# Attention and a top-2 mixture of experts on one core: a new order for the steps that find the row maxima

## The chip, the core and the metric

The kernel runs on one core of a Trainium2 chip. TensorE (PE) multiplies matrices, with weight loads shown apart as PEld; VectorE (DVE), ScalarE (ACT) and GpSimd (POOL) do elementwise work; SyncE (SP) issues DMAs. The metric is the device time of one execution in microseconds (us); lower is better.

## The reference

The input `x` has 8 batches of 1024 tokens of 256 numbers. All data are 32-bit floats.

```
x = x + layernorm(attention(layernorm(x)))      # 16 heads of 16, causal
x = x + layernorm(moe(layernorm(x)))            # 8 experts, top 2 per token

attention:  q, k, v = Wq x, Wk x, Wv x
            score = q k^T / 4, -inf above the diagonal
            out = Wo (softmax(score) v)
moe:        the 2 best experts of 8 by softmax(router)
            gate = min(gate, 7), up clipped to -7..7
            act = (up + 1) * gate * sigmoid(1.702 gate), then the down projection
            sum of the two, weighted by the router's scores
```

## The kernel before, in words

The program has two parts. The first, some 1400 us long, is the attention of all batches with the router; the second runs the experts over 142 tiles of 256 tokens. The change lies in the first part.

The attention is cut into 32 **units**: 8 batches times 4 groups of 4 heads (`u` counts units, `g = u % 4` is the group). A unit's 1024 x 1024 causal scores are computed twice. First, `maxima_tiles(u)` computes them with the queries in partitions (PSUM tile `sa`, line 689) and reduces them to a maximum for each row. Then the negated maxima go, transposed, into a spare row of the queries `qP`, so that when `values_tiles(u)` computes the scores again, with the keys in partitions (PSUM tile `sb`, line 784), the maximum is already subtracted and ScalarE has only to take the exponential (`pT`, line 792). The second pass of a unit runs one unit later than the first: in each iteration of the loop over `u`, the maxima of unit `u` and the exponentials of unit `u - 1` are worked at together.

**Steps and pairs.** Both passes go through 9 steps (`STEPS`, lines 631 to 643, `k` = 0 to 8), and each step handles two heads at a time (`pair` 0 and 1), the other pass taking the other two heads. A unit has so 18 pair-steps. In a pair-step TensorE makes 2 x 512 columns of scores for the maxima and 2 x 512 for the exponentials, in four different groups of 32 rows of the array; then half a step's products of `pT` with the values (`av`, line 821) for the step two before; then pieces of other work. A step is one of three kinds:

- EDGE: one query tile against the 512 keys at the diagonal. VectorE adds a mask and takes the maximum in one instruction per head (line 699).
- TWO: two query tiles whose causal widths add up to 512 (128 + 384, or 256 + 256). VectorE takes the maximum over the full blocks (line 714 or 720), and ScalarE copies the diagonal blocks out of PSUM into the tile `edge` (line 724). When both pairs are done, GpSimd masks `edge` (line 738) and VectorE reduces it (line 743).
- WHOLE: one query tile of the second 512 rows against all the first 512 keys; one reduction (line 705).

The kinds, in the order of `k`, are EDGE, TWO, TWO, EDGE, TWO, WHOLE, WHOLE, WHOLE, WHOLE. The TWO at `k` = 2, called "both" here, has one tile in each half (chunk `c`) of the rows. In the second pass every step but WHOLE has one or two diagonal blocks that GpSimd masks (line 801).

**The rows.** `rows(c)` sends the maxima of chunk `c` off when its last step has been counted: VectorE reduces and negates (`nm`, line 655), TensorE transposes (`nmps`, line 658), ScalarE copies (`nmT`, line 660), and four DMAs on SyncE's queue write the rows of `qP` (line 662). The chunk 0 rows can leave after "both"; the chunk 1 rows after the last WHOLE. The next unit's loop needs chunk 0 at step 0 and chunk 1 at step 2.

**The order of the work.** TensorE, VectorE, ScalarE and SyncE follow the order of the source. Pieces of other work (projections `pjq` and `pjk`, values `vps`, output projection `yps`, transposes `xps`, `aps`, `x2ps`, `avt`, the layer norms, the router) are placed by a small planner. Each pair-step earns credit for every engine (lines 1194 to 1200: 2.26 us less what the step itself takes), and a piece is placed when its turn has come and the engines that it needs have credit. Large pieces (1.75 us of TensorE) are placed ahead of a step's first `av` half (line 1206); when one is, and the step of `av` has one chunk only, both halves move to the second pair (`whole`). In pump, called at the end of each pair-step, small ones follow. `rows`, the mask jobs and `normalize` are "urgent" and come first.

**Buffers.** `sa` has two buffers of two PSUM banks. The pool `ps_b` has three of one bank: a pair-step's two `sb` tiles take two, and each piece of other work takes one.

**SyncE's queue.** `spread(u + 1)` (line 612) copies the next unit's queries and keys into `qP` and `kP`: two DMAs of zeros (line 617) and eight of data (line 620). It is called at the start of a unit, or at step 7 for the last group of a batch (line 1170). The queue holds also the `rows` DMAs, the loads of `x` (at step 5 of a batch's first unit) and the stores `x1d` (line 903).

Of the kernel before, what the change touches and what calls it, by code (L numbers as in the profile page):

```python
# [24 lines left out]
def piece(pe=0.0, dve=0.0, act=0.0, pool=0.0, after=0):  # L25


    return (pe, dve, act, pool), after
# [30 lines left out]
def attn_moe_kernel(  # L59
# [159 lines left out]
    def in_order(put, scatter=False):  # L219

        if free[0]:
            return
        for before_it in fixed if scatter else fixed + loose:
            tc.add_manual_dep(
                put.ins, before_it,
                mybir.DependencyInfo(mybir.DependencyClass.NoSync, mybir.DependencyReason.DATA),
                reason="order of the source",
            )
        if scatter:
            loose.append(put.ins.name)  # L230
        else:
            fixed[:], loose[:] = [put.ins.name], []
# [175 lines left out]
    with ExitStack() as attn:  # L408
# [219 lines left out]
        n = QC // P  # L628
        assert n == 4 and NC == 2
        WHOLE, EDGE, TWO = range(3)  # L630
        STEPS = []
# [10 lines left out]
        STEPS += [(WHOLE, [(n + i, 0, QC)], [(1, i, 0)]) for i in range(n)]  # L642
        K = len(STEPS)

        def maxima_tiles(u):

            b, g = divmod(u, NG)
            qP, kP = qPs[u % NU], kPs[u % NU]
            mx = mxs[u % 2]
            edges = {}  # L650

            def rows(c):
                yield piece(dve=0.2)
                nm = ap2.tile([P, HG, n], F32, tag="nm", name=f"nm_{u}_{c}")
                nc.vector.tensor_reduce(nm, mx[:, :, ts(c, n), :], AX.X, ALU.max, negate=True)
                yield piece(pe=0.15, act=0.3, after=1)
                ps = ps_b.tile([HG * n, P], F32, tag="b", name=f"nmps_{u}_{c}")
                nc.tensor.transpose(ps, nm.rearrange("p h i -> p (h i)"), ident)
                nmT = ap2.tile([HG * n, P], F32, tag="nmT", name=f"nmT_{u}_{c}")
                nc.scalar.copy(nmT, ps)  # L660
                for hh in range(HG):
                    nc.sync.dma_start(
                        out=qP[hh * HS + DH : hh * HS + DH + 1, ts(c, QC)].rearrange(
                            "o (i q) -> o i q", q=P
                        ),
                        in_=nmT[ts(hh, n), :],
                    )

            left = [
                sum(c in {i // n for i, _, _ in tiles} for _, tiles, _ in STEPS)  # L670
                for c in range(NC)
            ]

            def of_two(k):

                (i, _, w), (i2, _, _) = STEPS[k][1]
                return slice(i, i2 + 1, i2 - i), w == P

            def pair_of_heads(k, pair):
                kind, tiles, _ = STEPS[k]  # L680
                ps = ps_a.tile([P, 2, QC], F32, tag="a", name=f"sa_{u}_{k}_{pair}")

                def scores(hh, part):
                    if part == len(tiles):
                        return
                    i, c, w = tiles[part]
                    at = sum(t[2] for t in tiles[:part])
                    r = ds((2 * pair + hh) * HS, HS)
                    nc.tensor.matmul(  # L689
                        ps[:, hh, ds(at, w)], lhsT=qP[r, ts(i, P)], rhs=kP[r, ds(c * QC, w)],  # L690
                        start=True, stop=True,
                    )

                def reduce():
                    heads = ts(pair, 2)
                    i, c, w = tiles[0]
                    if kind == EDGE:
                        for hh in range(2):
                            nc.vector.tensor_tensor_reduce(  # L699
                                out=ps[:, hh, :], in0=ps[:, hh, :], in1=cmask,  # L700
                                scale=1.0, scalar=NEG, op0=ALU.add, op1=ALU.max,
                                accum_out=mx[:, 2 * pair + hh, i, 0:1],
                            )
                    elif kind == WHOLE:
                        nc.vector.tensor_reduce(mx[:, heads, i, 2:3], ps, AX.X, ALU.max)  # L705
                    else:
                        both, short = of_two(k)
                        if k not in edges:
                            edges[k] = ap2.tile(
                                [P, HG, 2, P], F32, tag="edge", name=f"edge_{u}_{k}"  # L710
                            )
                        blocks = ps.rearrange("p h (b k) -> p h b k", k=P)
                        if short:
                            nc.vector.tensor_reduce(  # L714
                                mx[:, heads, tiles[1][0], 0:1], ps[:, :, P : 3 * P],
                                AX.X, ALU.max,
                            )
                            at = blocks[:, :, 0:4:3, :]
                        else:
                            nc.vector.tensor_reduce(  # L720
                                mx[:, heads, both, 0], blocks[:, :, 0:4:2, :], AX.X, ALU.max
                            )
                            at = blocks[:, :, 1:4:2, :]
                        nc.scalar.copy(edges[k][:, heads], at)

                return scores, reduce

            def counted_off(k):
                for c in {i // n for i, _, _ in STEPS[k][1]}:
                    left[c] -= 1  # L730
                    if not left[c]:
                        rows_of[u, c] = start(urgent, rows(c))

            def masked_edges(k):

                d = edges.pop(k)
                yield piece(pool=1.25)
                in_order(nc.gpsimd.affine_select(
                    out=d, in_=d, compare_op=ALU.is_ge, fill=NEG,
                    base=0, pattern=[[0, HG], [0, 2], [-1, P]], channel_multiplier=1,  # L740
                ))
                yield piece(dve=1.2, after=1)
                nc.vector.tensor_reduce(mx[:, :, of_two(k)[0], 1], d, AX.X, ALU.max)
                counted_off(k)

            def done(k):
                if k in edges:
                    start(urgent, masked_edges(k))
                else:
                    counted_off(k)  # L750

            return pair_of_heads, done

        def values_tiles(u):
# [306 lines left out]
        def start(kind, gen):  # L1061
            job = Job(gen, now)
            kind.append(job)
            return job
# [70 lines left out]
        with tc.manual_schedule(  # L1135
# [11 lines left out]
            for u in range(B * NG + 1):  # L1147
                first = None
                if u < B * NG:
                    b, g = divmod(u, NG)  # L1150
                    if g == 1:
                        finish_by(jobs["v"], jobs["p1"])
                        if b + 1 < B:
                            jobs["x"] = start(due, prep(b + 1))
                    if g < NG - 1:
                        spread(u + 1)
                    if b + 1 < B and g == 2:
                        jobs["p0"] = start(due, project(b + 1, 0))
                    first = maxima_tiles(u)
                for k in range(K):  # L1160
# [15 lines left out]
                    for pair in range(2):  # L1176
# [15 lines left out]
                            use()  # L1192

                        us = 1.64 + 0.62
                        of_dve = {WHOLE: 1.22, EDGE: 1.68, TWO: 0.72}[STEPS[k][0]]
                        of_act = 1.8 if STEPS[k][0] == TWO else 1.2
                        share = 0.68, us - of_dve, us - of_act, us - 0.35
                        halves = (pair,) if first else (0, 1)
                        if first and second:
# [229 lines left out]
    with tc.manual_schedule(engines={engines.PE, engines.DVE, engines.Activation}):  # L1429
# [18 lines left out]
        for i in range(NTILES):  # L1448
# [4 lines left out]
            _, wg, bs, wd = loads.pop(i)  # L1453
# [71 lines left out]
```

## Time and profile before

| | |
|---|---|
| median of 3 runs | 2242.74 us (2240.94 to 2247.95) |
| profiled execution | 2242.13 us, span of its instructions 2240.4 us |
| granted TensorE clock | 0.987 |
| busy: PE / DVE / ACT / POOL | 97% / 73% / 49% / 48% of the span |
| scores of the maxima, L689 | 3072 matmul records, 659.7 us busy |
| scores for the exponentials, L784 | 3072 matmul records, 712.0 us busy |
| exponentials, L792 | 1152, 595 ns each |
| maxima of WHOLE, L705 | 256, 1218 ns each |
| maxima of EDGE, L699 | 256, 697 ns each |
| maxima of TWO, L714 | 128, 689 ns each |

A matmul of 32-bit floats shows as two records. The records overlap, and their ends are modelled, so the busy time of a line is no measure of what it costs; the distance between the starts of two pair-steps is. "Idle before" is the time that an engine stood still before an instruction, followed by what ended it.

### The profile page before, as it was taken

The numbers are of one execution on the slowest core, as the hardware profiler recorded it, in microseconds if no ns is written. First come the engines' busy times: TensorE is split into PE (matmuls) and PEld (weight loads), VectorE is DVE, ScalarE is ACT, GpSimd is POOL, SyncE is SP. The second block draws the span as 40 slices with busy tenths as digits, with TensorE's granted clock in tenths as the row PEclk, the third lists the DMA queues.
The fourth block names the chain that finished last, engine by engine and source line by source line (L and its number), as shares of the span: only waits on it lengthen the run. The fifth ranks groups of instructions, "written<-read, shape, count | busy, mean of one in ns | idle before, by whom it ended". The sixth has DMA issues, their size and how long they took to land.

```text
span 2240.4 us, 45184 instructions
## 1 busy us (share of the span) xinstructions
PE 2172.7 (97%) x16801; PEld 1356.0 (61%) x16801; DVE 1646.1 (73%) x3770; ACT 1090.1 (49%) x2179; POOL 1065.0 (48%) x1229
## 2 busy tenths in 40 slices
PE   7999999999999999999999999989999999999995
PEld 4444544544445445445445444678888888888884
DVE  3766777867777877877776787676658888887775
ACT  3566665666666666666666666422112322332222
POOL 3321553573473473472482463464445444454543
PEclk8899999999999999999999999999999999999998
DMA  3101102102111111111111111575567878877773
GB/s 82 38 4 40 22 20 59 40 21 53 37 29 38 51 30 34 51 35 26 51 42 21 47 51 40 205 230 207 201 219 264 274 252 272 275 243 274 242 245 121
DMA packets 141363, 251.17 MB, mean 112 GB/s; under 512 B 17664, under 2 KB 103576, under 8 KB 139224
## 3 DMA queue, kind: packets, MB, share of 16 engines
q1 hardware_dynamic: 127640, 212.22, 30.5%
q0 software_dynamic: 12960, 35.54, 4.2%
q8 instruction: 133, 2.18, 0.4%
q14 instruction: 86, 0.70, 0.1%
q10 hardware_dynamic: 544, 0.52, 0.1%
HBM read 175.74 MB, written 55.76 MB: 103 GB/s over the span
## 4 chain that ended last, share of the span: by engine, by line
PE 83%; DVE 8%; POOL 4%; issue 2%; ACT 1%; DMA 1%; SPq 1%; ACTq 0%; DVEq 0%; POOLq 0%
PE sa L689 20%; PE gu L1303 18%; PE av L821 12%; PE dn L1334 9%; PE sb L784 7%; PE vps L582 3%; PE yps L882 3%; PE pjk L596 3%; PE pjq L596 2%; PE avt L852 1%; PE xtps L1283 1%; DVE acc L1386 1%; POOL pT L801 1%; DVE gate L1312 1%; PE aps L872 1%
## 5 line engine op out<-in xcount | busy, mean ns | idle before, releaser
L792 ACT ACTIVATE pT<-sb 128x512 f32<-128x512 f32 x1152 | 625.0, 595 | 409.7 <-PE sb L784 380.1
L784 PE MATMUL sb<-qP,kP 32*128 32x512 f32 (+3 forms) x3072 | 712.0, 523 | 2.0 <-ACT pT L792 0.8
L689 PE MATMUL sa<-kP,qP 32*128 32x512 f32 (+3 forms) x3072 | 659.7, 527 | 3.2 <-DVE mx L699 1.4
L1303 PE MATMUL gu<-xsT,wg 128*128 128x256 f32 x2272 | 518.6, 381 | 0.7 <-ACT xsT L1285 0.7
L1303 PEld LDWEIGHTS gu<-xsT,wg 128*128 128x128 f32 x2272 | 432.9, 191 | 60.1 <-ACT xsT L1285 1.1
L801 POOL TENSOR_SCALAR_AFFINE_SELECT pT<-pT 128x512 f32<-128x512 f32 x256 | 159.6, 639 | 594.6 <-ACT pT L792 589.2
L1314 ACT ACTIVATE sig<-gate 128x256 f32<-128x256 f32 x284 | 118.3, 416 | 568.1 <-DVE gate L1312 565.2
L705 DVE TENSOR_REDUCE mx<-sa 128x2 f32<-128x1024 f32 x256 | 311.7, 1218 | 112.8 <-PE sb L784 108.7
L821 PE MATMUL av<-pT,vpad 128*32 128x256 f32 (+1 forms) x5120 | 345.0, 366 | 1.1 <-DVE avs L832 0.9
L689 PEld LDWEIGHTS sa<-kP,qP 32*128 32x128 f32 x3072 | 230.5, 185 | 189.8 <-issue 98.7
L1319 POOL TENSOR_TENSOR sig<-sig,gate 128x256 f32<-128x256 f32 x284 | 210.3, 742 | 279.7 <-ACT sig L1314 277.8
L784 PEld LDWEIGHTS sb<-qP,kP 32*128 32x128 f32 x3072 | 298.8, 184 | 40.0 <-ACT pT L792 7.5
L821 PEld LDWEIGHTS av<-pT,vpad 128*32 128x32 f32 x5120 | 116.3, 108 | 287.2 <-issue 209.1
L1334 PE MATMUL dn<-wd,act 128*128 128x256 f32 x1136 | 273.5, 382 | 8.3 <-DVE act L1324 7.8
L1312 DVE TENSOR_SCALAR gate<-gu,bs 128x256 f32<-128x256 f32 x284 | 135.7, 478 | 158.6 <-PE gu L1303 142.6
L1334 PEld LDWEIGHTS dn<-wd,act 128*128 128x128 f32 x1136 | 209.5, 191 | 39.9 <-DVE act L1324 14.6
L699 DVE CUSTOM_DVE_ANT_0 sa<-sa,cmask 128x512 f32<-128x512 f32 x256 | 178.1, 697 | 52.1 <-PE sb L784 27.4
L1344 POOL DMA_INDIRECT ytd<-ys,places x142 | 142.5, 1004 | 134.8 <-DVE ys L1340 109.2
L1042 POOL DMA_INDIRECT xsd<-xn,slots x128 | 126.3, 986 | 49.4 <-issue 30.3
L714 DVE TENSOR_REDUCE mx<-sa 128x2 f32<-128x512 f32 x128 | 88.2, 689 | 79.9 <-PE sb L784 49.7
L1324 DVE SCALAR_TENSOR_TENSOR act<-up,sig 128x256 f32<-128x256 f32 x284 | 130.3, 459 | 18.2 <-POOL sig L1319 18.2
L1316 DVE TENSOR_SCALAR up<-gu,bs 128x256 f32<-128x256 f32 x284 | 134.5, 473 | 0.0
(204 smaller groups left out, 2402.6 us busy)
## 6 DMA issues: line engine op xcount, KB each, us to landing
wg<-_L_ffn_gate_up_proj_dram SPq DMA_DIRECT2D x71, 1024.0 KB
wd<-in_L_ffn_down_proj_dram SPq DMA_DIRECT2D x71, 512.0 KB
xs<-xsd SPq DMA_DIRECT2D x67, 258.0 KB
yy<-ytd SPq DMA_DIRECT2D x15, 1024.0 KB
bs<-biasd SPq DMA_DIRECT2D x71, 132.0 KB
x<-in_L_attn_x_dram SPq DMA_DIRECT2D x16, 512.0 KB
x1d<-y SPq DMA_DIRECT2D x16, 512.0 KB
x<-x1d SPq DMA_DIRECT2D x16, 512.0 KB
```

Of the source, the lines that this page charges most:

```text
L689: nc.tensor.matmul(ps[:, hh, ds(at, w)], lhsT=qP[r, ts(i, P)], rhs=kP[r, ds(c * QC, w)], start=True, stop=True,)
L699: nc.vector.tensor_tensor_reduce(out=ps[:, hh, :], in0=ps[:, hh, :], in1=cmask, scale=1.0, scalar=NEG, op0=ALU.add, op1=ALU.max, accum_out ...
L705: nc.vector.tensor_reduce(mx[:, heads, i, 2:3], ps, AX.X, ALU.max)
L784: nc.tensor.matmul(banks[hh][:, ds(at, QC - off)], lhsT=kP[r, ts(j, P)], rhs=qP[r, ds(c * QC + off, QC - off)], start=True, stop=True,)
L792: nc.scalar.activation(pT[:, 2 * pair + hh, :], banks[hh], AF.Exp)
L801: in_order(nc.gpsimd.affine_select(out=d, in_=d, compare_op=ALU.is_ge, fill=0.0, base=0, pattern=[[0, HG], [1, P]], channel_multiplier=-1,))
L821: nc.tensor.matmul(av[ds(hh * HS, HS), ds(off + a - at, z - a)], lhsT=vp[:, j, ds((g * HG + hh) * VS, HS)], rhs=pT[:, hh, a:z],  start=c n ...
L1303: nc.tensor.matmul(ps[:, half, :], lhsT=wg[:, kt, ds(half * FF + f * P, P)], rhs=xT[:, kt, :], start=(kt == 0), stop=(kt == KT - 1),)
L1312: nc.vector.tensor_scalar(gt, ps[:, 0, :], bs[:, f : f + 1], LIMIT, ALU.add, ALU.min)
L1319: in_order(nc.gpsimd.tensor_tensor(sg, sg, gt, ALU.mult))
L1334: nc.tensor.matmul(ps[:, n, :], lhsT=act[:, f, ts(n, P)], rhs=wd[:, f, :], start=(f == 0), stop=(f == FT - 1),)
L1344: put = nc.gpsimd.indirect_dma_start(out=yt_dram[:, :], out_offset=bass.IndirectOffsetOnAxis(ap=places[:, i, n : n + 1], axis=0), in_=y[:, ...
```

## The change

The steps of the first pass get an order of their own, `A_STEPS`; the second pass keeps `STEPS`. Both still run in one loop over `k`.

| k | 0 | 1 | 2 | 3 | 4 | 5 | 6 | 7 | 8 |
|---|---|---|---|---|---|---|---|---|---|
| maxima before | EDGE | TWO | both | EDGE | TWO | WHOLE | WHOLE | WHOLE | WHOLE |
| maxima after | EDGE | TWO | WHOLE | EDGE | both | WHOLE | TWO | WHOLE | WHOLE |
| exponentials, before and after | EDGE | TWO | both | EDGE | TWO | WHOLE | WHOLE | WHOLE | WHOLE |

The number and the shape of the instructions stay as they are. The planner's credits for a pair-step (`of_dve`, `of_act`) follow the new order. The calls at fixed steps (`load_x` at 5, `spread` at 7) stay at their `k`.

```diff
         K = len(STEPS)
 
+
+        e0, t0, both, e1, t1, *rest = STEPS
+        A_STEPS = [e0, t0, rest[0], e1, both, rest[1], t1, rest[2], rest[3]]
+        assert len(A_STEPS) == K
+
         def maxima_tiles(u):
...
             left = [
-                sum(c in {i // n for i, _, _ in tiles} for _, tiles, _ in STEPS)
+                sum(c in {i // n for i, _, _ in tiles} for _, tiles, _ in A_STEPS)
                 for c in range(NC)
             ]
 
             def of_two(k):
 
-                (i, _, w), (i2, _, _) = STEPS[k][1]
+                (i, _, w), (i2, _, _) = A_STEPS[k][1]
                 return slice(i, i2 + 1, i2 - i), w == P
 
             def pair_of_heads(k, pair):
-                kind, tiles, _ = STEPS[k]
+                kind, tiles, _ = A_STEPS[k]
                 ps = ps_a.tile([P, 2, QC], F32, tag="a", name=f"sa_{u}_{k}_{pair}")
...
             def counted_off(k):
-                for c in {i // n for i, _, _ in STEPS[k][1]}:
+                for c in {i // n for i, _, _ in A_STEPS[k][1]}:
                     left[c] -= 1
                     if not left[c]:
                         rows_of[u, c] = start(urgent, rows(c))
...
                         us = 1.64 + 0.62
-                        of_dve = {WHOLE: 1.22, EDGE: 1.68, TWO: 0.72}[STEPS[k][0]]
-                        of_act = 1.8 if STEPS[k][0] == TWO else 1.2
+                        of_dve = {WHOLE: 1.22, EDGE: 1.68, TWO: 0.72}[A_STEPS[k][0]]
+                        of_act = 1.8 if A_STEPS[k][0] == TWO else 1.2
                         share = 0.68, us - of_dve, us - of_act, us - 0.35
```

## The prediction

> **What bounds the kernel now.** I read the page first, then the busy time by stretch, then the groups by shape inside the attention, then timelines.
>
> ```profile
> PE 2172.7 (97%) x16801; PEld 1356.0 (61%) x16801; DVE 1646.1 (73%) x3770; ACT 1090.1 (49%) x2179; POOL 1065.0 (48%) x1229
> ```
>
> ```profile
> 200.00:400.00 200.00, 199.69 (x1900) 93.96 (x1896) 146.90 (x304) 125.40 (x242) 87.25 (x97) 1.00 0.13 34
> 600.00:800.00 200.00, 198.68 (x1910) 95.73 (x1909) 151.97 (x334) 124.66 (x241) 109.95 (x121) 1.00 0.16 41
> ```
>
> In the attention (columns: length; busy PE, PEld, DVE, ACT, POOL; clock) TensorE is busy 99% of the time at full clock. But its ends are modelled, so I measured its waits otherwise: from the timeline I took the start of every pair-step in units 1 to 30, and subtracted from each distance the shortest time in which the same pieces are seen elsewhere (scores 1.07 us, one `av` half 0.57, two 1.00, four transposes 0.59, `nmps` 0.21, a large piece 1.92). The distances sum to 1273 us (68.1 to 1341.2), the pieces to 1197. So **76 us are waits, 2.5 us a unit**. No order can win more than that here; what it can lose is open.
>
> Where are they? By step and pair: step 0, second pair 11.7; step 2, first 9.2; step 4, 9.6 and 6.7; step 5, 7.8 and 4.0; none of the other twelve pair-steps has over 4.1. Step 4 of unit 19:
>
> ```profile
> 847.73 0.38 PE L689 MATMUL sa<-kP,qP 32*128 32x128 f32 x2
> ...
> 850.20 0.28 PE L658 MATMUL nmps<-ident,nm 128*16 128x128 f32 x1
> 850.32 0.66 PE L940 MATMUL x2ps<-ident,xn 128*128 128x128 f32 x4
> ...
> 850.91 0.38 PE L689 MATMUL sa<-kP,qP 32*128 32x128 f32 x2
> ...
> 851.11 0.25 ACT L660 COPY nmT<-nmps 16x128 f32<-16x128 f32 x1
> ...
> 851.38 2.57 SPq L662 DMA_DIRECT2D qP<-nmT  x4
> ...
> 853.04 0.66 PE L852 MATMUL avt<-ident,avs 128*128 128x128 f32 x4
> ...
> 853.62 0.70 PE L689 MATMUL sa<-kP,qP 32*128 32x512 f32 x2
> ```
>
> The first pair takes 3.18 us for 1.07 + 0.57 + 0.21 + 0.59 = 2.44; the second 2.71 for 2.23. `nmps`, x2ps and `avt` each take one of the three `ps_b` buffers that `sb` needs two of. `nmps` is given back only by `nmT`, which ScalarE reaches after the two exponentials and the edge copy. So chunk 0's `nmps` meets `avt`, which always falls in this step (all 30 units), or its neighbour. It starts in step 4's first pair in 15 units and in its second in 15. Of steps 4 and 5, all but the last 4.0 us (exponentials late after a TWO) are of this kind: **24 us**.
>
> **The change part by part.** *Instructions:* none added or removed, 0 us.
>
> *Unequal widths on TensorE.* WHOLE now runs beside "both" (k = 2), "both" beside 384 + 128 (k = 4), 128 + 384 beside WHOLE (k = 6). Before, the pairings that are not equal are 128 + 384 beside 384 + 128:
>
> ```profile
> 618.14 0.38 PE L689 MATMUL sa<-kP,qP 32*128 32x128 f32 x2
> 618.16 0.59 PE L784 MATMUL sb<-qP,kP 32*128 32x384 f32 x2
> 618.36 0.60 PE L689 MATMUL sa<-kP,qP 32*128 32x128 f32 x4
> 618.58 0.49 PE L784 MATMUL sb<-qP,kP 32*128 32x384 f32 x2
> ...
> 619.22 0.42 PE L821 MATMUL av<-pT,vpad 128*32 128x256 f32 x4
> ```
>
> All four scores take 1.08 us (618.14 to 619.22), as equal ones do: each row group goes on as it is free. The group at 618.36 holds two records of the `sa` tile's second part, issued behind `sb`'s first in the source, which started before the second pass of `sb` at 618.58. The Trainium skill's "TensorE: Matmul & The Clock Gate" (The mechanism) says that matmuls start and end strictly in order. By that, at k = 6 the 384 columns must wait for the second pass of the 512 beside them: the second pass starts 0.1 + 0.43 us in, where the row group is free at 0.1 + 0.21 = 0.32, so 0.21 us x 2 pairs x 31 units = **+13 us**. (An estimate from the trace: 512 columns take 1.07 - 0.1 in two passes, a first pass 0.1 more.) The trace shows no such wait, so the sum takes **0**; 13 goes into the range.
>
> *Chunk 0's rows* leave two steps later, as "both" moves from 2 to 4. From "both" to `nmps` it was two steps; I expect step 6, mostly its second pair. `avt` stays in step 4, since its order is the exponentials'. In step 6 a large piece stands in the first pair in 28 of 30 units, and then both `av` halves move to the second: 1.07 + 1.00 + 0.21 = 2.28 us, about what the two exponentials need to give their buffers back (1.07 + 0.1 + 1.09 = 2.26). There `nmps` costs nothing. Alone in a pair-step with one half (1.85 us) it costs about 0.4: that is chunk 1's `nmps` at step 0, whose wait is 11.7 / 30 = 0.39. I take two units in three at 0.1 and one at 0.55 (alone, or with a small transpose): 0.25 x 30 = 8 us. **-24 + 8 = -16 us.** From both sides: -24 if none is left, 0 if it meets xps and others as often.
>
> *VectorE at k = 2 and 6.*
>
> ```profile
> L705 DVE TENSOR_REDUCE mx<-sa 128x2 f32<-128x1024 f32 x236 | 287.4, 1218 | 109.7 <-PE sb L784 108.1
> L743 DVE TENSOR_REDUCE mx<-edge 128x8 f32<-128x1024 f32 x87 | 105.8, 1216 | 13.1 <-POOL edge L738 12.5
> L714 DVE TENSOR_REDUCE mx<-sa 128x2 f32<-128x512 f32 x118 | 81.3, 689 | 67.5 <-PE sb L784 49.4 <-PE sa L689 17.7
> ```
>
> A WHOLE costs 2 x 1.22 = 2.44 us; a TWO 2 x 0.69 and its mask's 1.22 one step later, 2.60. So the exchange moves 0.16 us. Over steps 2 and 3: before 1.38 + 3.36 (EDGE with its accumulator reads) + two masks' 2.43 = 7.2, after 2.44 + 3.36 + 1.22 = 7.0, both with 1.4 for the normalization, in 9.3 us. VectorE stands idle before L714 0.57 us each time and before L705 0.46: it waits for TensorE, not the reverse. 0, and if that slack were gone 0.53 us a pair-step.
>
> *ScalarE:* 2 x 0.59 of edge copies go from step 2 to 6, which has 5.0 us to step 2's 4.9. *GpSimd:* 1.12 us of edge mask leaves steps 2 to 4, where it also has seven of the eight `pT` masks (0.64 each), so `av` waits less. Together -2 to +2: 0.
>
> *SyncE's queue.* In unit 19 (last group) the order is rows, then `spread`:
>
> ```profile
> 831.18 22.77 SPq L662 DMA_DIRECT2D qP<-nmT  x8
> 854.00 1.23 SPq L617 DMA_DIRECT2D qP<-zeros  x2
> 855.27 2.93 SPq L620 DMA_DIRECT2D qP<-unq  x4
> 858.25 2.49 SPq L620 DMA_DIRECT2D kP<-unk  x4
> ```
>
> Each issue takes about 0.63 us, and what it carries is there 1.65 us after the issue began (in step 2 of unit 18 `sb` starts at 796.43 after the fourth rows issue at 794.77). The rows' four started 0.5 us into step 4's second pair; now I expect that at the start of step 7. Four and ten issues: the last key is there 0.5 + 13 x 0.63 + 1.65 = 10.3 us into step 7, and steps 7 and 8 take 9.1. But the next unit's first pair needs only the second of four keys, two issues (1.3) earlier: 9.0, just in time. Seven such changes of batch, 0 to 1 us late each: taken as **+2**. In other units chunk 0's rows have two pair-steps to spare; the `x` loads at step 5 put two issues (0.94 us in unit 16) before them: 0.
>
> *Chunk 1's rows* still leave after step 8. Sum -16 + 2 = **-14 us**. Against the profiled 2242.13 (span 2240.4 + 1.7 around it): 2228; the median is 0.6 above, so **2229**.
>
> **The rivals.** *The collision only moves* (22%). `nmps` meets xps or a large piece's copy, or TensorE keeps order after all (+13). Then -24 + 22 + 2 or so: 2236 to 2249, middle 2243. For it: small transposes fall in steps 5 to 8 too. Against: `avt` is the only one that is always there.
>
> *Chunk 1's rows slip* (slower, 28%). The last TWO's mask now falls in step 7, taking 1.2 us of VectorE's credit just ahead of `nm`. `nm` starts at step 0's first pair now in all units; if the mask's reduction comes as late as step 8's first pair, credit is negative at the end of step 8 and `nm` slips by a pair-step, 2.1 us. Step 2's first pair already waits 9.2 us for these DMAs, so a slip in half of the units is 16 x 2.1 = 34, less 14: +20, 2263. It decides from 10 slips (21 us) on for a measurable loss. For it: the chain is tight. Against: in step 6 a TWO leaves VectorE 1.54 us of credit a pair-step, so that the mask should run early in step 7.
>
> *The order does not take effect*: no; `maxima_tiles` reads A_STEPS throughout.
>
> **How the numbers follow.** This kernel's measurement tells about 0.3%, 6.7 us. Faster by more: 50% (the sum, 2212 to 2236: its best end is -24 and a few us of the others). Within: 22%. Slower: 28%. The range leaves out about a tenth at each end: 2212 to 2262.
>
> **What would show it.** In the changed profile: `nmps` of chunk 0 in step 6, not 4; waits in steps 4 and 5 down from 28 us to under 12; below 12 us in steps 6 and 7 together; 1.08 us for mixed scores; L705, L714 and L743 at the same durations. It is wrong if step 2's first pair waits over 15 us, if `sa` waits for VectorE in steps 2 to 4, or if a batch's first step waits over 2 us.

## The result, and the profile after

| | before | after |
|---|---|---|
| median | 2242.64 us (2240.94 to 2247.95) | 2251.82 us (2248.16 to 2253.64) |
| profiled execution | 2242.13 us, span 2240.4 | 2252.71 us, span 2251.0 |
| granted clock | 0.987 | 0.984 |

The change made the kernel slower: ratio 1.0036, 95% interval 1.0023 to 1.0049, some 9 us. The prediction said 2229. The second group of experiments below ran on a chip on which before takes 2243 us, as here. The other three ran on chips on which it takes 2277 us, the third and the fourth group on the same one. Each ratio is taken to before on the same chip.

First the page's line of busy time, then the same two stretches of the attention (length; busy PE, PEld, DVE, ACT, POOL; clock; DMA share; GB/s), of after:

```profile
PE 2177.5 (97%) x16801; PEld 1374.5 (61%) x16801; DVE 1653.5 (73%) x3770; ACT 1092.3 (49%) x2181; POOL 1066.3 (47%) x1229
```

```profile
200.00:400.00 200.00, 199.42 (x1887) 96.44 (x1879) 143.77 (x288) 125.74 (x242) 87.07 (x97) 1.00 0.11 28
600.00:800.00 200.00, 199.01 (x1890) 99.71 (x1883) 154.88 (x340) 125.61 (x244) 103.31 (x112) 0.99 0.14 36
```

Nothing here tells of a loss: the counts are the same, and TensorE is as busy as it was. The loss had to be placed by marks in the program. A mark is the first instruction of a unit or of an expert tile, read from the two traces:

| stretch | before | after | difference |
|---|---|---|---|
| start to unit 1 | 68.1 | 64.4 | -3.7 |
| units 1 to 30 | 1273.1 | 1274.1 | +1.1 |
| unit 31 to the first expert matmul `gu` | 73.7 | 73.3 | -0.4 |
| first `gu` to the start of expert tile 20 | 134.0 | 147.8 | **+13.8** |
| tile 20 to the end | 691.5 | 691.3 | -0.2 |

So the predicted 14 us are missing in the units, and 13.8 us are lost in a part that the change does not touch. (The start differs from profile to profile, with the old order too: unit 1 begins at 65.3 us in a later run of it.)

**In the units.** The timeline of after, unit 19: `avt` of step 4, then step 6's second pair and its `nmps`.

```profile
851.11 0.66 PE L857 MATMUL avt<-ident,avs 128*128 128x128 f32 x4
...
858.52 0.38 PE L694 MATMUL sa<-kP,qP 32*128 32x128 f32 x2
858.53 0.70 PE L789 MATMUL sb<-qP,kP 32*128 32x512 f32 x2
858.73 0.60 PE L694 MATMUL sa<-kP,qP 32*128 32x128 f32 x4
859.06 0.59 PE L789 MATMUL sb<-qP,kP 32*128 32x512 f32 x2
859.17 0.49 PE L694 MATMUL sa<-kP,qP 32*128 32x384 f32 x2
859.59 1.08 PE L826 MATMUL av<-pT,vpad 128*32 128x256 f32 x24
860.59 0.28 PE L663 MATMUL nmps<-ident,nm 128*16 128x128 f32 x1
```

`nmps` is where it was forecast, and scores of unequal widths (128 + 384 beside 512 + 512) still take 1.07 us, from 858.52 to 859.59: the first records of the 384 columns are in the group at 858.73, ahead of the second pass of `sb` at 859.06. In all units the median is 1.10, 1.08 and 1.07 us at steps 2, 4 and 6. The maxima's reductions take what they took (from the costliest groups of after's page):

```profile
L710 DVE TENSOR_REDUCE mx<-sa 128x2 f32<-128x1024 f32 x256 | 312.0, 1220 | 79.1 <-PE sb L789 75.0
L719 DVE TENSOR_REDUCE mx<-sa 128x2 f32<-128x512 f32 x128 | 88.4, 691 | 103.4 <-PE sb L789 82.6
```

The waits, worked out as in the prediction, in us by step (both pairs):

| step | 0 | 1 | 2 | 3 | 4 | 5 | 6 | 7 | 8 | sum |
|---|---|---|---|---|---|---|---|---|---|---|
| before | 14.2 | 7.2 | 11.5 | 6.1 | 16.3 | 11.8 | 1.4 | 3.4 | 4.3 | 76.2 |
| after | 17.3 | 9.2 | 10.5 | 2.3 | 7.3 | 8.6 | 5.9 | 5.7 | 12.1 | 78.6 |

Steps 4 and 5 gave 12 us, steps 6 and 7 took 7 back, step 8's second pair and step 0's first took 15 (from 6.6 to 21.3). The last lie nearly all where one batch follows another. SyncE's queue at such a place (unit 15 to 16), before:

```profile
678.77 2.62 SPq L662 DMA_DIRECT2D qP<-nmT  x4
681.75 1.25 SPq L617 DMA_DIRECT2D qP<-zeros  x2
```

and after, where step 7 starts at 688.03 us and unit 16 at 698.21:

```profile
679.29 0.34 SPq L908 DMA_DIRECT2D x1d<-y  x1
688.63 2.57 SPq L667 DMA_DIRECT2D qP<-nmT  x4
691.25 1.23 SPq L617 DMA_DIRECT2D qP<-zeros  x2
...
695.76 2.48 SPq L620 DMA_DIRECT2D kP<-unk  x4
```

and what TensorE's first scores of unit 16 wait for (the second line is the weight load of the other head):

```profile
698.21 1.29 PE L694 MATMUL sa<-kP,qP 32*128 32x512 f32 x3 [0.99 <-DVE counted L1011]
698.81 0.18 PEld L694 LDWEIGHTS sa<-kP,qP 32*128 32x128 f32 x1 [0.33 <-DMA kP<-unk]
```

The queue stands still from 679.6 to 688.63 for `nmT`, and the ten transfers of `spread` behind it leave only then. The first pair-step of unit 16 needs the first two of its four keys. They were issued at 695.76 and 696.39, and the scores that need them start at 698.21 and 698.81. (The first line names an instruction of VectorE; that the queue is the cause was tried, see the second group.) The large piece after these scores then runs at half clock for 2.8 us. In all, 3.4 us are lost at this change of batch.

**In the expert part.** The same stretch, first `gu` to tile 20, of before and then of after (columns as above, with the instructions counted), and below each the transpositions `x2ps` that routing needs, 8 records for each chunk of 512 tokens (duration min/median/max, first and last start, from 1400 us on):

```profile
1414.90:1548.90 134.00, 121.88 (x599) 103.50 (x600) 94.76 (x289) 40.44 (x82) 71.45 (x81) 0.96 0.68 230
```

```profile
L940 PE MATMUL x2ps<-ident,xn x16: 272/273/332, 1443.6 to 1456.5; 128*128 128x128 f32 x16
```

```profile
1411.90:1559.70 147.80, 128.49 (x627) 106.80 (x628) 99.78 (x322) 44.59 (x88) 76.21 (x86) 0.94 0.59 196
```

```profile
L945 PE MATMUL x2ps<-ident,xn x24: 272/414/477, 1419.4 to 1506.6; 128*128 128x128 f32 x24
```

16 records before, 24 after: of the 16 chunks, two are still to be routed when the experts start before, three after. Chunks 12 and 13 were both routed around the start of unit 31 before (1338.3 to 1350.3); after, chunk 13 is the third left over. The stretch holds 28 more matmul records and 33 more of VectorE, and is 13.8 us longer, 6.6 of it as busy TensorE and 7.2 as idle. From tile 20 on, all is as before. The trace also shows how it came to be late. In batches 2 to 5 (of 0 to 7), `x2ps` of both chunks of a batch ran within 18 us before (660.1 to 678.1); after, the second chunk's start 67 to 70 us behind the first's (669.2 and 738.8).

### The profile page after: what moved, and what is told of

It is laid out like the page before. It is cut to its first block, busy times and chain, and to the rows that moved or that the text cites. A ratio compares the mean times of both kernels' runs of the same rounds, so it can differ in the third digit from the quotient of the medians.

```text
span 2251.0 us, 45075 instructions
## 1 busy us (share of the span) xinstructions
PE 2177.5 (97%) x16801; PEld 1374.5 (61%) x16801; DVE 1653.5 (73%) x3770; ACT 1092.3 (49%) x2181; POOL 1066.3 (47%) x1229
## 3 DMA queue, kind: packets, MB, share of 16 engines
q8 instruction: 133, 2.18, 0.4%
## 4 chain that ended last, share of the span: by engine, by line
PE 85%; DVE 7%; POOL 3%; issue 2%; DMA 1%; ACT 1%; SPq 1%; ACTq 0%; DVEq 0%; POOLq 0%
PE sa L694 20%; PE gu L1308 17%; PE av L826 13%; PE sb L789 9%; PE dn L1339 8%; PE vps L582 3%; PE pjq L596 3%; PE pjk L596 3%; PE yps L887 3%; PE avt L857 2%; DVE acc L1391 1%; POOL xsd L1047 1%; PE xtps L1288 1%; DVE gate L1317 1%; PE x2ps L945 1%
## 5 line engine op out<-in xcount | busy, mean ns | idle before, releaser
L710 DVE TENSOR_REDUCE mx<-sa 128x2 f32<-128x1024 f32 x256 | 312.0, 1220 | 79.1 <-PE sb L789 75.0
L743 POOL TENSOR_SCALAR_AFFINE_SELECT edge<-edge 128x1024 f32<-128x1024 f32 x96 | 106.8, 1112 | 206.3 <-ACT edge L729 206.3
L719 DVE TENSOR_REDUCE mx<-sa 128x2 f32<-128x512 f32 x128 | 88.4, 691 | 103.4 <-PE sb L789 82.6
L1329 DVE SCALAR_TENSOR_TENSOR act<-up,sig 128x256 f32<-128x256 f32 x284 | 129.9, 457 | 24.8 <-POOL sig L1324 24.6
```

## The experiments

**First group, on a chip at 2277 us.** Theory T: the loss is the routing that is left over. Rival W: it comes from waits inside the units.

*The new order in units 0 to 7 only.* The planner keeps its lag to the end: three chunks are left.

```diff
+        def steps_of(u):
+            return NEW_STEPS if u < 8 else STEPS
```

> The new order in units 0 to 7 alone, the old one in units 8 to 31. Theory T (late routing): the new order costs nothing inside the units; it makes the planner place the second chunk's layer norm and routing of each batch later, and this lag stays with the planner's state once it is there. In this kernel's instruction order three chunks are left to route when the attention ends, as in the changed kernel, against two in the kernel before, although 24 units have the old order. T expects the last scatter (xsd) near 1540 us instead of 1497, and a time 8 to 14 us above the kernel before: 2250 to 2256. Rival W (waits inside the units, above all at the changes of batch, where spread comes late): the loss goes with the number of units in the new order, a quarter of 9 us: 2243 to 2246.

Measured: 2292.82 us, ratio 1.0059 (1.0038 to 1.0081), 15.7 us over before, where T has 8 to 14 and W up to 3; first `gu` to tile 20 150.2 us. Against the run of before's order below, units 1 to 30 are 2 us longer and this stretch 12.5. So the loss doesn't grow with the units in the new order.

*"both" moved, the last TWO at step 5.* This order leaves two chunks.

```diff
-[e0, t0, rest[0], e1, both, rest[1], t1, rest[2], rest[3]]
+[e0, t0, rest[0], e1, both, t1, rest[1], rest[2], rest[3]]
```

> Half of the change: the step called both goes from 2 to 4 and a WHOLE from 5 to 2, while the last TWO goes only from 4 to 5, so that two TWO steps stand side by side (EDGE, TWO, WHOLE, EDGE, both, TWO, WHOLE, WHOLE, WHOLE). Chunk 0's rows leave as late as in the changed kernel. In the instruction order two chunks are left to route at the end of the attention, as before. Theory T: no loss in the tail, so at or below the kernel before, 2232 to 2244. Rival W: chunk 0's rows are late on the queue of SyncE just the same, so the changes of batch wait some 15 us as in the changed kernel, and the time is about that of the changed kernel, 2249 to 2254.

Measured: 2290.0 us, ratio 1.0054 (1.0036 to 1.0072). The stretch to tile 20 is short, 127.7 us, as T says of two chunks; but the first `gu` starts only at 1469.1 us, 21 us later than in the run of before's order below. The total missed both forecasts: on this chip the units lose something that the first chip did not show.

*The changed kernel, and before, with 16 early tiles.* Tiles from `EARLY` on are found in the last chunk's table.

```diff
-    EARLY = 12
+    EARLY = 16
```

> The changed kernel with EARLY at 16 instead of 12: four more expert tiles run from the table of the first 12 chunks, so that tile 16 instead of tile 12 is the first that needs the last table. Theory T: what costs the changed kernel its time is that tiles from 12 on wait for the last table, 43 us later than before; with four tiles more (some 25 us of work) most of that wait goes: 2239 to 2246. Rival W: the time was lost in the attention, and nothing changes: 2249 to 2254.

> The kernel before with EARLY at 16 instead of 12. Theory T: it waits little for its last table (tile 12 takes 12.6 us against some 9), so it gains less than the changed kernel does: 2236 to 2243, and stays within 5 us of the changed kernel with EARLY at 16. Rival W: unchanged within 3 us, and the changed kernel with EARLY at 16 stays 9 us above it.

Measured: after 2316.98 us, ratio 1.0182 (1.0145 to 1.022), stretch 150.9 us; before 2281.93 us, 1.0019 (1.0007 to 1.0031), stretch 137.7 us. A form of T falls here: if the tiles from 12 on waited for the last table, four more early ones would have helped. The two runs lie 35 us apart, where T has up to 5 and W has 9, so both missed; of the 30 us between their profiles, 16 are in units 1 to 30 and 13 in the stretch. What stays is that three chunks left go with a long stretch (147.8, 150.2, 150.9), two with a short one (134.0, 127.7, 137.7).

**Second group, on a chip at 2243 us.** Here the number of chunks left is changed by itself, in both orders, by the start of one chunk's output projection in batch 6.

*The changed kernel again,* as the yardstick.

> The changed kernel once more, beside the before on this chip, as the yardstick for the three others. Theory T (the loss lies in the expert part: three chunks, 13 to 15, are still to be routed when the attention ends, where before two are, and the third costs 13 to 16 us between the first `gu` and the start of expert tile 20): that stretch near 148 us, and 8 to 14 us over before in all if the attention costs what it did on the first chip. Rival W (the loss lies in the waits inside the attention's units, and the expert part only follows): the start of the first `gu` later than before by at least the whole difference.

Measured: 2250.1 us, ratio 1.0035 (1.0023 to 1.0047), stretch 147.8 us, first `gu` at 1409.6. The first result once more: 6.9 us over before, a little under the 8 to 14 expected.

*The old order with three chunks left.*

```diff
         def finish(b, c):
+            if b == 6 and c == 1:
+                yield piece(after=8)
```

> The kernel before, old order of the maxima in all units; only the second chunk of batch 6 starts its output projection 8 pair-steps later, so that three chunks are left to route at the end of the attention instead of two. Nothing is left out of the computation. Theory T: the stretch from the first `gu` to tile 20 grows from 134 to 147-151 us, the first `gu` starts up to 3 us sooner (one chunk's routing less in the attention), total 10 to 15 us over before, as slow as the changed kernel. Rival W: the order is the old one, so total within 3 us of before.

Measured: 2250.62 us, ratio 1.0034 (1.0021 to 1.0047). **The old order is as slow as the new one once three chunks are left.** The stretch has the matmul and VectorE counts of after and is 3.6 us shorter than there; `x2ps` has 24 records, as after:

```profile
1415.30:1559.50 144.20, 128.50 (x627) 107.54 (x628) 99.46 (x322) 44.00 (x88) 74.27 (x84) 0.94 0.65 217
```

```profile
L942 PE MATMUL x2ps<-ident,xn x24: 272/273/330, 1417.6 to 1503.0; 128*128 128x128 f32 x24
```

That is 10.2 us over before, and the attention is not shorter for the routing that it no longer holds (first `gu` at 1415.3, before 1414.9). In the median it is 7.4 us. T had 10 to 15 in all and 147 to 151 for the stretch, W at most 3 in all: T's sizes were somewhat too large.

*The new order with two chunks left.*

```diff
         def finish(b, c):
+            if b == 6 and c == 0:
+                yield piece(after=14)
```

> The changed kernel, new order in all units; only the first chunk of batch 6 starts its output projection 14 pair-steps later, which gives chunk 13 its turn before the end of the attention, so that two chunks are left as before. Nothing is left out. Theory T: first `gu` to tile 20 back from 148 to 131-138 us, total 8 to 13 us less than the changed kernel on this chip, that is about before or up to 3 us under it. Rival W: total as the changed kernel within 3 us, since its units are the same up to the last four.

Measured: 2236.69 us, ratio 0.9972 (0.9963 to 0.998), 13.4 us under the changed kernel beside it (T has 8 to 13, W 3) and 6.5 under before. The stretch:

```profile
1409.90:1547.60 137.70, 124.31 (x607) 104.86 (x608) 94.11 (x295) 40.56 (x82) 74.50 (x85) 0.96 0.70 228
```

```profile
L947 PE MATMUL x2ps<-ident,xn x16: 272/273/421, 1447.6 to 1459.4; 128*128 128x128 f32 x16
```

295 instructions of VectorE in place of 322, and 10.1 us less. The units are as in after: 75.8 us of waits. So W is out for this loss, and T is shown from both sides.

*Besides, the rows behind `spread`.* In a batch's last group chunk 0's four DMAs come three pair-steps later.

```diff
                 nc.scalar.copy(nmT, ps)
+                if c == 0 and g == NG - 1 and b + 1 < B:
+                    yield piece(after=3)
```

> As the one with two chunks left, and besides, in the last group of each batch, chunk 0's four DMAs of rows wait 3 pair-steps, so that they stand behind the ten of `spread` on SyncE's queue and no longer before them. The trace of the changed kernel shows 9.2 us in step 0's first pair and 12.1 in step 8's second, against 2.5 and 4.1 before, nearly all at the seven changes of batch. If the queue's order is their cause: 6 to 12 of these 14.7 us go, and total is 6 to 12 us under the one with two chunks left. If their cause is VectorE's routing pieces in front of `sa` there: within 3 us of it.

Measured: 2222.14 us, ratio 0.9912 (0.99 to 0.9925), more than was expected. Its SyncE queue at the same change of batch (step 7 starts at 678.05, unit 16 at 687.17):

```profile
669.67 1.29 SPq L617 DMA_DIRECT2D qP<-zeros  x2
...
674.01 2.49 SPq L620 DMA_DIRECT2D kP<-unk  x4
678.65 3.05 SPq L669 DMA_DIRECT2D qP<-nmT  x4
```

`spread` now leaves 8.4 us ahead of step 7, where in after it left 3.2 us into it. Step 8's second pair and step 0's first hold 8.3 us of waits (20.5 in the kernel without this edit), all units 61.8 us. So these waits come from the queue's order, and not from VectorE's routing pieces, with which they would have stayed. They come to 12 us. In the median 14.5 us were won, between the two profiles 21.2; what these have beyond the units, 2.3 in the start and 4.8 in the stretch to tile 20, was not followed.

**Third group, at 2277 us.** Is it the order that wins in the units, or only the later `nmps`? Theory M: only `nmps`. Rival O: the order.

*The old order, `nmps` of chunk 0 four pair-steps later,* and then *the same with the rows behind `spread`* (the edit above):

```diff
-                yield piece(pe=0.15, act=0.3, after=1)
+                yield piece(pe=0.15, act=0.3, after=1 if c else 5)
```

> The kernel before, old order of the maxima in all units; only the transposition `nmps` of chunk 0 waits 4 pair-steps more, so that it falls where the new order puts it (step 6). Two chunks are left at the end of the attention. Nothing is left out. Theory M (what the new order wins is only that `nmps` no longer meets `avt` in step 4; what it loses in the units is only that chunk 0's row DMAs and `spread` come later at a change of batch): waits of steps 4 and 5 fall from 28 to 12-18 us, waits of step 8's second pair and step 0's first rise from 7 to 15-22 us, total within 6 us of before, like the changed kernel with two chunks left (2 to 9 us under before). Rival O (the order itself, a WHOLE beside both and the mask in another step, is what counts): steps 4 and 5 keep over 22 us and total is 0 to 10 us over before.

> The same, and in a batch's last group chunk 0's four row DMAs wait 3 pair-steps more, behind the ten of `spread`. Theory M: the 14.7 us at the changes of batch are not there, total 15 to 22 us under before (ratio 0.990 to 0.9935), the same as the new order with these two changes. Rival O: at least 8 us slower than the new order with them.

Measured: 2269.04 us, ratio 0.9961 (0.995 to 0.9972), and 2253.43 us, ratio 0.9898 (0.9876 to 0.992). In the first, step 8's second pair and step 0's first hold 20.6 us, as M says; steps 4 and 5 hold 24.0 us, which is O's forecast (over 22) and not M's, but 7.7 of that are the chip's waits told of below. The total is 8.3 us under before, where O has 0 to 10 over. With later rows the queue's order is worth 15.6 us in the old order as well.

*The half change and the best version so far, on this chip:*

> Half of the change: `both` goes from step 2 to 4, but the TWO of step 4 goes to 5 and not to 6, so that two TWO steps stand next to each other; with the row DMAs behind `spread` in a batch's last group. Two chunks are left. Theory M: the place of the last TWO is worth nothing, total within 4 us of the full order with two chunks left and the rows behind (ratio 0.990 to 0.993). Rival O: two neighbouring TWO steps crowd the edge copies and masks, 5 to 15 us slower than it (ratio 0.9935 to 0.998).

> The new order with two chunks left and the rows behind `spread`, once more, beside the three others on this chip: ratio to before 0.990 to 0.9925 as measured. Should the chip be a slower one with late semaphores of TensorE in the attention, the ratio may be worse, and then the three others are to be read against this one.

Measured: 2266.36 us, ratio 0.9949 (0.993 to 0.9968), and 2279.16 us, ratio 1.0008 (0.9997 to 1.0018). The version that was 0.9% faster than before on the other chip gains nothing here. Beside it the half change is 13 us faster, and the old order with both edits 26 us faster. M has 0 to 4 us between them, O has the new order ahead by 5 or more: both missed.

**Fourth group, meant for a chip at 2243 us, but again at 2277 us.**

> Old order, chunk 0's `nmps` 4 pair-steps later, and its row DMAs behind `spread` at a change of batch, once more. Theory M (only the place of `nmps` counts): ratio 0.990 to 0.9935 on either kind of chip, and on one with before near 2243 us within 4 us of the new order with the two repairs. Rival O (the order itself counts): on a chip at 2243 us 6 us or more slower than the new order. Late reports, if the chip has them, can move both by 10 to 20 us, and then the waits by pair-step decide.

> New order, two chunks left, rows behind `spread`, a third time. On a chip at 2243 us: ratio 0.990 to 0.9925 as the first time; on one at 2277 us: 0.9995 to 1.002 as the second.

> `both` at step 4 and the last TWO at 5, rows behind `spread`, once more. Theory M: on a chip at 2243 us within 4 us of the full order with the two repairs (0.990 to 0.993). Rival O: 5 us or more slower. On a chip at 2277 us: 0.993 to 0.997 as measured.

> The changed kernel as it is. On a chip at 2243 us: ratio 1.0023 to 1.0049, as measured twice. On a chip at 2277 us: its repaired version lost 0.96% there against the other chip, so 1.010 to 1.016.

Measured ratios: old order with later rows behind `spread` 0.9951 (0.9936 to 0.9967); best version 1.0066 (1.0043 to 1.0089); half change 1.0005 (0.9995 to 1.0015); the changed kernel 1.0152 (1.0133 to 1.0172), as expected of it. The other three lie above what was expected of them. Each of these three is 0.5 to 0.6% slower than it was in the third group, on the same chip and with before at 2277 us both times, and their intervals don't meet: an interval does not cover what changes from one group of runs to the next. So the change costs 0.35% on one kind of chip and 1.5% on the other.

What differs is seen in the same pair-steps of the same kernel, the best version, unit 20, step 4. On the chip at 2243 us (start, duration; in brackets the idle time before and what ended it):

```profile
876.70 0.60 PE L696 MATMUL sa<-kP,qP 32*128 32x256 f32 x4
...
877.34 0.69 DVE L727 TENSOR_REDUCE mx<-sa 128x4 f32<-128x512 f32 x1 [0.17 <-PE sb L791]
877.47 1.08 ACT L799 ACTIVATE pT<-sb 128x512 f32<-128x512 f32 x2 [1.08 <-PE sb L791]
```

and on one at 2277 us:

```profile
900.03 0.60 PE L696 MATMUL sa<-kP,qP 32*128 32x256 f32 x4
...
903.39 0.69 DVE L727 TENSOR_REDUCE mx<-sa 128x4 f32<-128x512 f32 x1 [2.89 <-PE av L828]
...
904.18 1.09 ACT L799 ACTIVATE pT<-sb 128x512 f32<-128x512 f32 x2 [4.47 <-PE sa L696]
```

TensorE does its scores and goes on with a projection and `av` at the same distances in both. But VectorE begins 0.64 us after these scores' start in the one and 3.36 us in the other, ScalarE 0.77 and 4.15. Both wait there for TensorE's semaphore (a counter by which it reports). Its next four increments are in the trace at 876.89, 877.32, 877.36 and 877.40 in the one, and at 902.60, 903.37, 904.08 and 904.12 in the other: the scores are reported late. Then the next scores wait for their buffers. In both traces GpSimd is issuing the scatters `xsd` of a routed chunk at that moment.

I took all pair-steps of units 2 to 29 that waited over 1 us. In the six profiles on chips at 2243 us, before among them, none of 34 lies within 6 us after or 4 us before the start of a scatter; in eleven of the twelve profiles at 2277 us 151 of 198 do (in the twelfth, the new order in units 0 to 7, 17 of 21), and these hold 25 to 57 us a profile. They are most of what the units hold more on such a chip: without them, the waits of the best version are 67.2 and 65.4 us in its two runs at 2277 us, 61.8 on the other kind of chip; of the old order with later rows behind `spread`, 58.5 and 72.7; of the half change, 59.7 and 60.9. Two profiles of one kernel differ by up to 14 us, more than the three kernels do, so here the runs don't tell the orders apart.

But the order has a part in the waits near scatters themselves: they hold some 26 and 33 us in the old order with later rows behind `spread`, 35 and 47 in the half change, 40 and 57 in the best version. So M holds at most for the waits that are left without them, within some 14 us. In the totals the order counts on this chip, by 26 and 28 us, and the other way round than O has it. That the scatters are the cause was not tried (no run left them out), nor the old order with later rows on a chip at 2243 us.

## Why the prediction was wrong

Profile against profile, the prediction had 2228.1 us (2242.1 less 14) and 2252.7 were measured. Of the 24.6 us between them, 15.1 lie in units 1 to 30 (1.1 us longer, for 14 shorter), 13.8 in the stretch to tile 20, and -4.3 in the rest.

- *The sum ended at the units.* It covered TensorE, VectorE, ScalarE, GpSimd and SyncE within a unit and had no term for what the planner does with the other work. That the credits follow the new order stands in the description of the change; what they place was taken to be placed in time all the same. It was not: chunk 13's routing slid over the end of the attention, and that costs 10 us (10.2 and 10.1 in the two pairs that change nothing else), 13.8 in the first comparison. This is the step that failed, a term that was left out, and no rival had it. The two steps that follow are the 15 us in the units: terms that were there, but mis-sized. Which of the shifted credits starts the lag was not settled; the new order in eight units is enough.
- *SyncE's queue, +2.* The mechanism was named, the rows ahead of `spread`, and the time of the rows right (the start of step 7: 688.63 against 688.03). The size was off: 15 us for 2. It was right that the first pair-step needs only the second of the four keys. But that key was taken to be there 1.65 us after its issue, a figure read off the rows; at the seven changes of batch its score starts 2.4 to 2.5 us after it. The first issue comes 0.6 us into step 7, not 0.5. So even the four changes without further trouble lose 1.2 to 1.8 us each, not 0 to 1. In the other three the issues of `spread` take 0.7 to 1.2 us longer in all (over the 13 issues at unit 16, 0.69 on average, not 0.63), and two of them then run into a stretch at half clock: 2.0 to 4.1 us each.
- *Chunk 0's rows, -16.* Steps 4 to 7 together went from 32.9 to 27.5: -5. Steps 4 and 5 came down to 15.9, not to 4: half of the 24 us that were laid to `nmps` stay without it. That all of it was of one kind was read off one example; what the other half waits for was not found. Steps 6 and 7 took back 6.8, where 8 was forecast.
- *Chunk 1's rows unchanged; the rival that they slip.* Right to leave it out: step 2's first pair fell from 9.2 to 5.8, and chunk 1's `nm` starts no later than step 0's first pair in any unit. The `nmps` of chunk 1 did slip to step 0's second pair in nine units (before: in one), mostly a batch's first, but step 2's first pair waits 0.3 us or less in them. The old order with later rows slips in the same nine, so the last TWO is not the cause.
- *Unequal widths 0, and not +13.* Right: 1.07 us. The strict order that the Trainium skill's "TensorE: Matmul & The Clock Gate" (The mechanism) states does not show in this trace.
- *Instructions, VectorE, ScalarE and GpSimd at 0.* L710, L719 and L748 at 1220, 691 and 1214 ns for 1218, 689 and 1216. All waits of steps 2 to 4 together fell from 33.9 to 20.1 us. From 100 to 1350 us TensorE stood idle for a maximum of VectorE once, 0.5 us (before: twice, 0.9).
- *Its own checks.* `nmps` in step 6: yes (30 of 30 units). Steps 6 and 7 under 12: yes, 11.6. Steps 4 and 5 under 12: no, 15.9. And "a batch's first step waits over 2 us", named as what would make it wrong, came true in unit 12, with 2.18.

With both faults mended the units hold 61.8 us of waits, 14.4 under before: the sum of the prediction, but from other places (steps 0 to 3 give 11 of them, steps 4 to 7 5.5, step 8 takes 2). That such a sum comes true does not prove its terms.

## What to carry to other kernels

Where a planner fills gaps by credit, a new order moves other work too: list which jobs are left when the stage ends, before and after, and follow them into the next stage. In an in-order queue a transfer that is not yet due blocks all that could leave behind it; put those with ready data first. A gain of under 1% on one chip should be measured on a second one, and again on the first. A wait seen in one example should be counted in all units before its whole group is laid to it.

## What was not expected of the hardware

**A stretch at half clock follows a short idle time.** At the change of batch from unit 11 to 12, after:

```profile
522.50:526.00 3.50, 1.85 (x17) 0.97 (x14) 3.00 (x12) 1.08 (x2) 3.34 (x3) 1.00 0.58 101
526.30:529.70 3.40, 3.40 (x11) 1.63 (x10) 1.52 (x4) 1.09 (x2) 0.00 (x0) 0.50 0.37 68
```

TensorE was busy for 1.85 of 3.5 us, and then ran 3.4 us at a granted clock of 0.50. The Trainium skill's "TensorE: Matmul & The Clock Gate" (What's actually happening) gives windows of about 3.4 us and half rate after an idle one; the length agrees, but here a window with half of its time idle was enough. Before has no such stretch between 100 and 1400 us, after three (526, 700 and 1328), the old order with three chunks left three as well, the best version at 2243 us none. By an estimate from the trace, such a wait costs up to 1.7 us (half of 3.4) on top of itself. In the twelve profiles at 2277 us, units 1 to 30 hold 10 to 61 us at half clock; by the same estimate 5 to 31 us of their waits are this.

**Late reports.** That the same instructions on two chips differ by 3 us in when one engine hears of another, mostly near scatters, was not known from before's trace. The waits there hold 25 to 57 us of a profile. With them the new order with both mends goes from 0.9% under before on one chip to 0.1% (within the noise) and 0.7% over it on another. What makes the chips differ stays open.
